# Group-norm chains shared between channel blocks and images, and some of them moved between stages, in a four-layer convolution kernel

## The chip, the cores and the metric

One core of a Trainium2 chip runs the whole network in one launch, in float32. The metric is device time in microseconds (us). Five engines run side by side, each through its own queue in order: PE (matmul; its weight loads are shown as PEld), DVE (vector), ACT (activation), POOL (GpSimd) and SP (only issues DMAs here). An engine waits for another by semaphore, and an instruction that waits holds up all that is queued behind it on its engine.

## The reference

Four layers, each of the form x = x + layer(groupnorm(x)), on x of shape (4, 256, 56, 56). Layers 0 and 2 are involutions, layer 1 is two 3x3 convolutions, layer 3 is a gate. What the change touches is the group norm:

```python
def _gn(v, G=32, eps=1e-5):
    g = v.reshape(B_, G, C_ // G, H_, W_)
    m = jnp.mean(g, axis=(2, 3, 4), keepdims=True)
    s = jnp.var(g, axis=(2, 3, 4), keepdims=True)
    return ((g - m) / jnp.sqrt(s + eps)).reshape(v.shape)

x = x + _L0_conv_ref(_gn(x), ...)   # involution: 7x7 kernels of every pixel, made by two 1x1 products
x = x + _L1_conv_ref(_gn(x), ...)   # conv3x3, bn, relu, conv3x3, bn, relu(x + h)
x = x + _L2_conv_ref(_gn(x), ...)   # involution with batch norms
x = x + _L3_conv_ref(_gn(x), ...)   # x * sigmoid gate of the channel + x * real DFT of the channel mean
```

A group is 8 channels of one image, so the mean and variance of one image and one block of 128 channels are 16 groups on 128 partitions.

## The kernel before

**Units.** A unit is one image and one block of 128 channels; there are 8 in a layer, unit u = 2 * image + block. An involution works through them one by one. Each unit has two stages. The *tap stage* (`tap_matrices`) has 32 steps: PE makes products of the span weights with the bottleneck's output (L594) into one of four two-bank PSUM buffers, and DVE (L612, two steps of three) or ACT (L605, every third step, those with n % 3 == 2) moves them with a bias into `kt`. The *column stage* has 7 columns: PE applies `kt` to the windows of the column (`apply`, L636), ACT and DVE combine the parts (L649 or L651, L656), the residual is added (POOL L661 in layer 0, DVE L663 in layer 2), PE transposes the next strip of the image (L408), and POOL or ACT makes the strip after that (L393, L391).

**Chains.** The group norm of one unit is a chain, the generator `norm_steps` (L212 to L236): `bn_aggr` of the statistics (DVE L216), a matmul that averages the means over 8 channels (PE L219), copy, subtract, square, add (DVE L222 to L227, four instructions in one step), a second matmul (PE L230), + eps (DVE L150), to the power -0.5 (POOL L151), and the shift (DVE L234): six steps, every operand 128 x 1. Each matmul takes one of the four PSUM buffers until DVE has read it. There are 32 chains, 8 for each of the four norms, and norm n + 1 of a unit needs the sums that layer n's columns leave behind (`column_sums`, L1106).

**Order.** All instructions of a layer keep the order in which the program writes them, on each engine (`in_order`). What is done beside a stage is placed by hand: `hooks[n]` is called after tap step n, `late[tx]` after column tx, and one call advances a generator by one step. Before the change, the chains stand like this:

- Layer 0, units 1 to 7: the last column's sums of the unit before at hook 1, its chain for norm 1 at hooks 2, 6, 7, 11, 12, 13.
- Layer 0, units 1, 3, 5 (block 1 of images 0 to 2): also the chain for norm 0 of the next image's block 0, at hooks 15, 19, 20, 24, 25, 26; the statistics for it (`sums`, L361) come one to a column in the column stage before. The next image's block 1 has its chain in columns 1 to 3 of units 1, 3, 5, and `bottleneck` of the next image follows there.
- Layer 1 (`conv_layer`): unit 7's chain for norm 1 at the start, and for norm 2 of images 0 to 2 two chains each, one per block, stepped through the second convolutions by `in_groups`.
- Layer 2, units 1 to 7: the chain for norm 3 of the unit before at hooks 2, 6, 7, 11, 12, 13, and `channel_mean` of that unit at hooks 13 (DVE L697, L708) and 17 (PE L716, L719). Units 1 and 2 also hold the chains for norm 2 of the last image, at hooks 15 to 26.
- Layer 2, units 3, 5, 7: POOL gate chunks (`gate_chunk`, L804 to L817) of the image before at hooks 14, 18, 22, 26. Units 2, 4, 6 have `gate_factors` at hooks 24 to 31.

Of the kernel before, what the change touches and what calls it, by code (L numbers as in the profile page):

```python
# [10 lines left out]
F32 = mybir.dt.float32  # L11
# [5 lines left out]
P = 128  # L17
# [56 lines left out]
def net_kernel(  # L74
# [70 lines left out]

    mhalf = const.tile([P, NB], F32, name="mhalf")
    nc.gpsimd.memset(mhalf, -0.5)
# [56 lines left out]

    norm_sb = const.tile([P, 4, B, 2, NB], F32, name="norm_sb")
    norms = [[[norm_sb[:, i, b, k, :] for k in range(2)] for b in range(B)] for i in range(4)]

# [3 lines left out]

    def norm_steps(st, one_bank, layer, b, cb):  # L212

        rstd, shift = (t[:, cb : cb + 1] for t in norms[layer][b])
        mv = small.tile([P, 2], F32, name="mv")
        nc.vector.bn_aggr(mv, st)  # L216
        yield
        ps = one_bank()
        nc.tensor.matmul(ps[:, 0:1], gavg_sb, mv[:, 0:1], start=True, stop=True)  # L219
        yield  # L220
        gm = small.tile([P, 1], F32, name="gm")
        nc.vector.tensor_copy(gm, ps[:, 0:1])  # L222

        d = small.tile([P, 1], F32, name="d")
        nc.vector.tensor_sub(d, mv[:, 0:1], gm)
        nc.vector.tensor_mul(d, d, d)
        nc.vector.tensor_add(d, d, mv[:, 1:2])  # L227
        yield
        ps = one_bank()
        nc.tensor.matmul(ps[:, 0:1], gavg_sb, d, start=True, stop=True)  # L230
        yield
        rsqrt_eps(rstd, ps[:, 0:1], GN_EPS)
        yield
        nc.vector.scalar_tensor_tensor(shift, gm, -1.0, rstd, ALU.mult, ALU.mult)  # L234
        yield

    redn_of = {}
# [63 lines left out]
    def involution_layer(layer, xin, xout, red, span, sb, xs_of, ahead=None, pending=None):  # L301

        with ExitStack() as es:
# [24 lines left out]
            if layer == 0:  # L328
                load(0, 0, (2, 2, 2, 1))
                load(0, 1, (2, 2, 2, 1))  # L330

                nc.scalar.activation(norm_sb[:, 3, B - 1, 1, :], mhalf, AF.Sigmoid)
            z_sb = wpool.tile([P, G // 2, ZN], F32, name="z_sb")
# [163 lines left out]
            def begin():  # L497
# [25 lines left out]
                steps(sums0, NCHUNK)  # L523
                norm = norm_steps(sums_of[0, 0], lambda: bank, 0, 0, 0)
                steps(norm, 2)
# [9 lines left out]
                steps(sums1, NCHUNK - 4)  # L535
                norm = norm_steps(sums_of[0, 1], lambda: bank, 0, 0, 1)

# [425 lines left out]

            def norm_of(layer, b, cb, st):
                return norm_steps(st, one_bank, layer, b, cb)

# [52 lines left out]
            for u, (b, cb) in enumerate(units):  # L1019
                hooks = hooks0 if u == 0 else {}  # L1020
                if prev is not None:
                    pb, pc, st, last_sums = prev
                    hooks.setdefault(1, []).append(last_column(last_sums))
                    place(hooks, norm_of(layer + 1, pb, pc, st), (2, 6, 7, 11, 12, 13))
                    if layer == 2 and u < 3:
                        g = norm_of(2, B - 1, u - 1, pending[1][u - 1])
                        place(hooks, g, (15, 19, 20, 24, 25, 26))
                    if layer == 2:
                        place(hooks, channel_mean(pb, pc), (13, 17))
                        if pc == 1:  # L1030
# [16 lines left out]
                if layer == 0 and cb == 1 and b + 1 < B:  # L1047
                    place(hooks, norm_of(0, b + 1, 0, sums_of[b + 1, 0]), (15, 19, 20, 24, 25, 26))

# [13 lines left out]
                if b + 1 < B:  # L1063
                    if layer == 0:
                        g = sums(b + 1, cb)
                        if cb == 0:
                            for tx in range(NTX):
                                late[tx].append(step(g))
                        else:
# [3 lines left out]
                            def norm_last():  # L1073
                                yield from norm_of(0, b + 1, 1, sums_of[b + 1, 1])

# [14 lines left out]
                if layer == 2 and b > 0:  # L1090
                    if cb == 0:
                        late[0] += [lambda b=b, j=j: load_sf(b - 1, j) for j in range(2)]
                    for tx in range(1, 6) if cb == 0 else range(NTX - 2):
                        late[tx] += [next_load, next_gate]
                if last_image and cb == 0:
                    for tx in range(6):
# [28 lines left out]
            if layer == 2:  # L1125
                run(last_normed(b, 0))
                bank = one_bank()
                mean, norm = last_mean(b, bank), norm_steps(st, lambda: bank, 3, b, cb)
                warm(16, ident_sb)
# [54 lines left out]
    def conv_layer(xin, xout, st, ahead):  # L1184
        with ExitStack() as es:
# [613 lines left out]
            def in_groups(g):  # L1799

                for n in (0, 0, 1, 1, 1, 0, 1, 1, 1):
                    for _ in range(n):
                        next(g, None)
                    yield
# [47 lines left out]

            tail1, tail2, slow = [], [], [in_groups(norm_steps(st, lambda: spare[0], 1, B - 1, NB - 1))]
            for s, (conv, i) in enumerate(order):
# [47 lines left out]
                else:  # L1902
# [60 lines left out]
                    if i % 3 == 0 and i > 0:  # L1963

                        slow += [in_groups(norm_steps(sums_of[i // 3 - 1][co], lambda: spare[0], 2, i // 3 - 1, co)) for co in range(NB)]
                    if nxt == (2, n_chunks - 1):
                        after[2].append(ahead)
                    between = [[] for _ in range(NB)]
                    for n, g in enumerate(slow[-NB:]):
                        between[n].append(step(g))  # L1970
# [86 lines left out]
```

## Time and profile before

| what | us |
|---|---|
| three timed runs | 1674.44, 1679.3, 1685.94 (median 1679.3) |
| the profiled execution, its own time | 1677.15 |
| its span, first to last instruction | 1675.3 |
| layer 0: first tap step to last column | 44 to 505 |
| layer 1 between the involutions | 505 to 1139 |
| layer 2: first tap step to last column | 1139 to 1642 |

A line of the profile gives an engine, a line of the kernel, the operation, and the tile it writes <- the tiles it reads. In a timeline the first two numbers are the start and the length in us, x is how many instructions were merged, and the square brackets give how long the engine had been idle and who ended that. A float32 matmul is two records, so a tap step of six products has twelve.

### The profile page before, as it was taken

The numbers are of one execution on the slowest core, as the hardware profiler recorded it, in microseconds if no ns is written. First come the engines' busy times: TensorE is split into PE (matmuls) and PEld (weight loads), VectorE is DVE, ScalarE is ACT, GpSimd is POOL, SyncE is SP. The second block draws the span as 40 slices with busy tenths as digits, with TensorE's granted clock in tenths as the row PEclk, the third lists the DMA queues.
The fourth block names the chain that finished last, engine by engine and source line by source line (L and its number), as shares of the span: only waits on it lengthen the run. The fifth ranks groups of instructions, "written<-read, shape, count | busy, mean of one in ns | idle before, by whom it ended". The sixth has DMA issues, their size and how long they took to land.

```text
span 1675.3 us, 57542 instructions
## 1 busy us (share of the span) xinstructions
PE 1601.8 (96%) x24640; PEld 1449.8 (87%) x24640; DVE 1333.5 (80%) x2451; ACT 1010.1 (60%) x2203; POOL 557.1 (33%) x774
## 2 busy tenths in 40 slices
PE   6999999999999999999999999988999899899898
PEld 4998998998888899899999999968888878788776
DVE  2686787787668988999999999986867777777775
ACT  2655555556446566676666666427776576676654
POOL 2134223322422343433333333100001581581571
PEclk9999999999998999999999999998999999999996
DMA  2354445444558977987888788653544774873752
GB/s 92 121 184 120 157 148 178 135 149 137 180 169 264 169 138 149 200 184 162 173 170 169 146 174 164 144 163 124 171 135 153 226 218 154 244 210 125 209 169 104
DMA packets 102876, 275.68 MB, mean 165 GB/s; under 512 B 15877, under 2 KB 43790, under 8 KB 98910
## 3 DMA queue, kind: packets, MB, share of 16 engines
q0 software_dynamic: 43856, 106.25, 30.8%
q1 hardware_dynamic: 57726, 164.48, 30.5%
q8 instruction: 195, 3.19, 0.8%
q10 hardware_dynamic: 1040, 1.26, 0.3%
q14 instruction: 59, 0.48, 0.1%
HBM read 95.07 MB, written 49.15 MB: 86 GB/s over the span
## 4 chain that ended last, share of the span: by engine, by line
PE 63%; DVE 16%; issue 7%; DMA 6%; ACT 5%; POOL 2%; SPq 1%; ACTq 0%; POOLq 0%; DVEq 0%
PE mm L1569 18%; PE ps L594 15%; PE ps L636 13%; PE mm L1554 7%; DVE kt L612 6%; DMA xw<-xw 4%; DVE un L656 3%; PE ps L408 3%; PE ps L470 1%; DVE st L1106 1%; ACT hp L489 1%; DVE xs L663 1%; DMA xs<-v 1%; ACT xw L420 1%; PE ps L719 1%
## 5 line engine op out<-in xcount | busy, mean ns | idle before, releaser
L636 PE MATMUL ps<-kt,xw 126*32 126x48 f32 (+1 forms) x12544 | 382.3, 236 | 21.9 <-DMA xw<-xw 9.4
L636 PEld LDWEIGHTS ps<-kt,xw 126*32 126x32 f32 (+1 forms) x12544 | 343.1, 122 | 68.0 <-issue 44.0
L594 PE MATMUL ps<-hp,z_sb 64*126 64x133 f32 x6144 | 384.9, 279 | 9.6 <-DVE kt L612 5.6
L594 PEld LDWEIGHTS ps<-hp,z_sb 64*126 64x126 f32 x6144 | 364.8, 186 | 26.0 <-DVE kt L612 7.7
L612 DVE TENSOR_TENSOR kt<-ps,zb_sb 126x798 f32<-126x798 f32 x352 | 333.2, 981 | 60.2 <-PE ps L594 48.8
L605 ACT ACTIVATE kt<-ps,zb_sb 126x133 f32<-126x133 f32 x960 | 280.3, 441 | 110.4 <-PE ps L594 110.4
L1569 PE MATMUL mm<-xs,u_sb 128*128 128x140 f32 (+2 forms) x1664 | 208.6, 278 | 1.7 <-DMA xs<-v 1.7
L1569 PEld LDWEIGHTS mm<-xs,u_sb 128*128 128x128 f32 x1664 | 199.4, 191 | 2.1 <-issue 1.7
L1554 PE MATMUL mm<-v,u_sb 128*128 128x280 f32 (+2 forms) x864 | 194.2, 383 | 2.0 <-DVE hp L1585 2.0
L1554 PEld LDWEIGHTS mm<-v,u_sb 128*128 128x128 f32 x864 | 162.2, 190 | 27.7 <-issue 2.4
L656 DVE SCALAR_TENSOR_TENSOR un<-ps,s,un 128x240 f32<-128x240 f32 x224 | 102.5, 457 | 88.1 <-ACT un L651 84.1
L656 DVE SCALAR_TENSOR_TENSOR un<-ps,par_sb,un 128x240 f32<-128x240 f32 x224 | 97.8, 456 | 82.5 <-ACT un L649 78.4
L1537 POOL DMA_DIRECT2D xs<-v x100 | 96.9, 1006 | 173.9 <-ACT xs L1536 161.2
L661 POOL TENSOR_TENSOR xs<-un,xs 128x240 f32<-128x240 f32 x112 | 72.2, 665 | 217.2 <-DVE un L656 217.2
L151 POOL TENSOR_TENSOR norm_sb<-norm_sb,mhalf 128x1 f32<-128x1 f32 x32 | 19.5, 609 | 344.0 <-DVE norm_sb L150 344.0
L420 ACT COPY xw<-ps 126x896 f32<-126x896 f32 x112 | 101.3, 905 | 40.9 <-PE ps L408 21.8
L649 ACT ACTIVATE un<-ps,par_sb 128x240 f32<-128x240 f32 x112 | 50.2, 448 | 120.0 <-PE ps L636 111.5
L408 PE MATMUL ps<-ident_sb,strip_sb 128*126 128x128 f32 x784 | 112.8, 285 | 6.3 <-POOL strip_sb L393 2.2
L651 ACT ACTIVATE un<-ps,bn_t,s 128x240 f32<-128x240 f32 x112 | 60.0, 538 | 92.0 <-PE ps L636 84.0
L408 PEld LDWEIGHTS ps<-ident_sb,strip_sb 128*126 128x126 f32 x784 | 85.7, 143 | 17.6 <-issue 3.9
L1569 PE MATMUL mm<-v_sb,u_sb 128*128 128x140 f32 (+2 forms) x688 | 94.2, 279 | 1.8 <-ACT u_sb L1316 1.8
L1536 ACT ACTIVATE xs<-v 128x560 f32<-128x560 f32 (+2 forms) x100 | 61.7, 628 | 49.5 <-DVE v L1481 41.6
(325 smaller groups left out, 2437.4 us busy)
## 6 DMA issues: line engine op xcount, KB each, us to landing
xw<-xw SPq DMA_DIRECT2D x224, 252.0 KB
xw<-xw SPq DMA_DIRECT2D x224, 126.0 KB
xs<-x POOLq DMA_DIRECT2D x24, 560.0 KB, 6.9
x<-xs POOLq DMA_DIRECT2D x8, 1568.0 KB, 8.1
xs<-x SPq DMA_DIRECT2D x8, 1568.0 KB
xs<-v POOLq DMA_DIRECT2D x44, 280.0 KB, 4.5
xs<-v POOLq DMA_DIRECT2D x42, 252.0 KB, 4.3
xs<-in_x_dram SPq DMA_DIRECT2D x6, 1568.0 KB
```

The costliest lines, as they stand in the source:

```text
L408: nc.tensor.transpose(ps[:Q, k * P : (k + 1) * P], flat[:, k * Q : (k + 1) * Q], ident_sb)
L420: nc.scalar.copy(xw[:, :NSB, :], ps[:Q, : NSB * P].rearrange("q (n c) -> q n c", n=NSB))
L594: nc.tensor.matmul(ps[:Q, i, k * NT : (k + 1) * NT], z_sb[i * R : (i + 1) * R, cb * GB // 2 + gp, z0 : z0 + Q], hp[i * R : (i + 1) * R, py ...
L605: nc.scalar.activation(kt[:, g0 + i, pb, :, k], ps[:Q, i, k * NT : (k + 1) * NT], AF.Identity, bias=zb_sb[:, cb * GB + g0 + i, p0 + k : p0 ...
L612: nc.vector.tensor_tensor(kt[:, g0 : g0 + 2, pb], ps[:Q, :, : PB * NT].rearrange("q i (k t) -> q i t k", k=PB), zb_sb[:, cb * GB + g0 : cb ...
L636: nc.tensor.matmul(v[m * j : m * j + m, i, :, k * TP : (k + 1) * TP], xw[:, window(ty), m * j : m * j + m], kt[:, ng * j : ng * j + ng, :, ...
L656: nc.vector.scalar_tensor_tensor(part, o[e], s, part, ALU.mult, ALU.add)
L661: nc.gpsimd.tensor_tensor(dst, u, dst, ALU.add)
L1536: nc.scalar.mul(t[:, at], v[:, below], -1.0)
L1537: nc.gpsimd.dma_start(t[:, at], v[:, at], accum_op=ALU.add)
L1554: nc.tensor.matmul(ps, *position(u, v, ci, dy, k, co, n), start=(j == 0), stop=(j == NB * 3 - 1))
L1569: nc.tensor.matmul(ps[:, bank, co * m : (co + 1) * m], u[ci][:, co * P : (co + 1) * P], v2[:, : n // 2, ci * WT : (ci + 1) * WT], start=(c ...
```

## The change

All chains work on several units at once if asked: the statistics of all 8 units stand in one tile `mv_sb`, the scales and shifts of one norm are contiguous over the units, and a chain takes a range u0:u1. Each small operation is now a step of its own (nine steps instead of six); where the six old steps are wanted, `by_counts` bundles them again.

```diff
-    norm_sb = const.tile([P, 4, B, 2, NB], F32, name="norm_sb")
+    norm_sb = const.tile([P, 4, 2, B * NB], F32, name="norm_sb")
+    mv_sb = const.tile([P, 2, B * NB, 2], F32, name="mv_sb")
...
+    def norm_steps(sts, one_bank, layer, u0, u1):
+        rstd, shift = (norm_sb[:, layer, k, u0:u1] for k in range(2))
+        mean, var = (mv_sb[:, layer % 2, u0:u1, k] for k in range(2))
+        for u, st in sts.items():
+            aggregate(st, layer, u)
         yield
         ps = one_bank()
-        nc.tensor.matmul(ps[:, 0:1], gavg_sb, mv[:, 0:1], start=True, stop=True)
+        nc.tensor.matmul(ps[:, :n], gavg_sb, mean, start=True, stop=True)
         yield
...
         nc.vector.tensor_copy(gm, ps[:, :n])
+        yield
         nc.vector.tensor_sub(d, mean, gm)
+        yield
         nc.vector.tensor_mul(d, d, d)
+        yield
         nc.vector.tensor_add(d, d, var)
         yield
...
+    def by_counts(g, counts):
+        for n in counts:
+            for _ in range(n):
+                next(g, None)
+            yield
```

In the involutions:

```diff
-                    hooks.setdefault(1, []).append(last_column(last_sums))
-                    place(hooks, norm_of(layer + 1, pb, pc, st), (2, 6, 7, 11, 12, 13))
-                    if layer == 2 and u < 3:
-                        g = norm_of(2, B - 1, u - 1, pending[1][u - 1])
-                        place(hooks, g, (15, 19, 20, 24, 25, 26))
+                    hooks.setdefault(5 if layer == 0 else 1, []).append(last_column(last_sums))
                     if layer == 2:
-                        place(hooks, channel_mean(pb, pc), (13, 17))
+                        place(hooks, norm_of(3, {u - 1: st}, u - 1, u), (2, 6, 8, 9, 10, 11, 13, 15, 16))
+                        place(hooks, channel_mean(pb, pc), (17, 18))
+                    else:
+                        hooks.setdefault(8, []).append(lambda st=st, u=u: aggregate(st, layer + 1, u - 1))
...
                 if layer == 0 and cb == 1 and b + 1 < B:
-                    place(hooks, norm_of(0, b + 1, 0, sums_of[b + 1, 0]), (15, 19, 20, 24, 25, 26))
+                    place(hooks, first, (5,))
...
                         if cb == 0:
-                            for tx in range(NTX):
+                            for j in range(NCHUNK + 1):
+                                late[j // 2].append(step(g))
+                            def norm_first():
+                                yield from norm_of(0, {u + 2: sums_of[b + 1, 0]}, u + 2, u + 3)
+                            g = first = norm_first()
+                            for tx in (3, 4, 5, 5, 5, 5, 6, 6):
                                 late[tx].append(step(g))
...
                 if last_image and cb == 0:
+                    g = by_counts(norm_of(1, {}, 0, u), (1, 1, 4, 1, 1, 1))
+                    for tx in range(1, 7):
+                        late[tx].append(step(g))
+                if layer == 2 and u == 0:
+                    g = by_counts(norm_of(2, dict(enumerate(pending[1], NB * (B - 1))), NB * (B - 1), NB * B), (1, 1, 4, 1, 1, 1))
+                    for tx in range(1, 7):
+                        late[tx].append(step(g))
```

So norm 1 of units 0 to 5 becomes one chain in the columns of unit 6, and units 6 and 7 share one in layer 1; in layer 1 the two blocks of an image share a chain for norm 2, and the two chains of the last image become one in the columns of unit 0 of layer 2:

```diff
-                        slow += [in_groups(norm_steps(sums_of[i // 3 - 1][co], lambda: spare[0], 2, i // 3 - 1, co)) for co in range(NB)]
+                        u = NB * (i // 3)
+                        sts = dict(enumerate(sums_of[i // 3 - 1], u - NB))
+                        slow.append(in_groups(norm_steps(sts, lambda: spare[0], 2, u - NB, u)))
...
-                    for n, g in enumerate(slow[-NB:]):
+                    for n, g in enumerate(slow[-1:]):
```

32 chains become 22.

## The prediction

> **What bounds the kernel now.** I read the page's busy table and the chain of waits first:
>
> ```profile
> PE 1601.8 (96%) x24640; PEld 1449.8 (87%) x24640; DVE 1333.5 (80%) x2451; ACT 1010.1 (60%) x2203; POOL 557.1 (33%) x774
> ...
> PE 63%; DVE 16%; issue 7%; DMA 6%; ACT 5%; POOL 2%; SPq 1%; ACTq 0%; POOLq 0%; DVEq 0%
> PE mm L1569 18%; PE ps L594 15%; PE ps L636 13%; PE mm L1554 7%; DVE kt L612 6%; DMA xw<-xw 4%; DVE un L656 3%; PE ps L408 3%; PE ps L470 1%; DVE st L1106 1%; ACT hp L489 1%; DVE xs L663 1%; DMA xs<-v 1%; ACT xw L420 1%; PE ps L719 1%
> ```
>
> PE sets the end nearly everywhere, so an edit is worth what it takes out of PE's row or out of waits of PE. Only in the tap stages does DVE (L612) stand beside it in the chain. So next I cut the span into tap stages, from the first L594 to the first L636 (busy time of each engine by stretch; first number the length). The first three are units 2, 3 and 4 of layer 0, the last unit 3 of layer 2:
>
> ```profile
> 164.20:188.97 24.77, 24.62 (x396) 23.79 (x396) 22.65 (x33) 18.42 (x61) 3.40 (x5) 1.00 0.47 166
> 217.66:244.27 26.61, 25.95 (x401) 24.59 (x400) 24.09 (x41) 18.43 (x61) 3.93 (x6) 1.00 0.49 168
> 280.35:305.12 24.77, 24.62 (x397) 23.79 (x396) 22.67 (x33) 18.43 (x61) 3.38 (x5) 1.00 0.46 164
> ...
> 1325.20:1353.05 27.85, 26.99 (x419) 24.43 (x418) 24.42 (x39) 20.54 (x64) 14.05 (x21) 1.00 0.59 198
> ```
>
> Units 2 and 4 hold one chain, unit 3 two: the trace has the experiment in it. A second chain costs 26.61 - 24.77 = 1.84 us. PE's timeline of unit 4 shows where one goes:
>
> ```profile
> 280.35 5.12 PE L594 MATMUL ps<-hp,z_sb 64*126 64x133 f32 x84
> 285.40 0.38 PE L219 MATMUL ps<-mv,gavg_sb 128*128 128x1 f32 x2
> 285.94 3.69 PE L594 MATMUL ps<-hp,z_sb 64*126 64x133 f32 x60 [0.15 <-DVE kt L612]
> 289.56 0.38 PE L230 MATMUL ps<-d,gavg_sb 128*128 128x1 f32 x2
> 289.87 14.39 PE L594 MATMUL ps<-hp,z_sb 64*126 64x133 f32 x240
> 304.20 0.98 PE L408 MATMUL ps<-ident_sb,strip_sb 128*126 128x128 f32 x7
> ```
>
> L219 to the next L594 is 0.54 us (in it a wait for DVE to free a buffer, since the chain holds one of four), L230 to the next 0.31, and the steps around them are slower.
>
> **Layer 0, tap stages.** Without a chain: layer 2's first tap stage has none, and its gapless run of 20 steps from 1151.75 to 1165.64 gives 13.89 / 20 = 0.695 us a step. 32 of them are 22.2; about 0.2 for switching weights at both ends and 0.84 for the transposes that stand before L636 make 23.3. So a lone chain costs 24.77 - 23.3 = 1.45 us. Seven stages (units 1 to 7) lose it: 10.2. Three (units 1, 3, 5) lose a second one: 3 x 1.84 = 5.5. Sum **-15.7**. What stays on DVE: the last column's sums (0.62, now hook 5), `bn_aggr` (0.34, hook 8), in three units one shift (0.16). DVE was busy for 22.67 of 24.77; without six small operations (about 1.0) it needs 21.7 of 23.3, so it has room, but little. I charge 0.1 a stage, **+0.7**; the bounds are 0 and the whole 0.96 of DVE time, which I don't take because in unit 4 the same two instructions stand at hooks 1 and 2 and L594 runs on without a gap to step 6.
>
> **Layer 0, columns.** Three chains (next image, block 0) and the six-unit chain go there. The trace has such a chain already, that of the next image's block 1. Three columns in a row, without a chain, with L219, with L230:
>
> ```profile
> 251.37:255.50 4.13, 4.13 (x119) 3.73 (x119) 4.03 (x10) 1.74 (x3) 2.28 (x3) 1.00 0.61 187
> 255.50:260.29 4.79, 4.29 (x127) 4.00 (x121) 3.91 (x12) 1.80 (x3) 2.16 (x3) 1.00 0.65 206
> 260.29:264.70 4.41, 4.28 (x128) 4.00 (x121) 2.61 (x11) 1.80 (x3) 2.77 (x5) 1.00 0.55 162
> ```
>
> 0.66 + 0.28 = 0.94 us. The block 0 chain has its second matmul behind the last column, ahead of tap step 0, where the buffer wait (0.50 before L636 at 257.10) may come twice: bounds 0.94 and 1.45, I take 1.2. 3 x 1.2 + 0.95 = **+4.5**. Six columns of operands instead of one change nothing: the instructions' length is fixed cost (a 128x1 DVE operation takes 0.15, L716 with 1 column 0.18). The sums (L361), now two to a column, cost nothing: the column at 251.37 holds three and is 4.13 long. If that cover went, 7 x 0.6 us a unit in three units would show. POOL gets three L151 of 0.56 behind strips (0.99 each) in columns where it is busy for 2.3 of 4.1. Layer 0: -15.7 + 0.7 + 4.5 = **-10.5**.
>
> A rule to weigh against the row of L219: the Trainium skill ("TensorE: Matmul & The Clock Gate", section "Wait — 56ns, not 53.3ns?") gives small matmuls a floor of about 25 ns from start to start; by it a chain's four records would be 0.1 us of PE and ten chains about 1 us, an estimate that speaks against any visible gain. The stages' difference of 1.84 us says that a chain's price is the switch and the buffer, not the matmul.
>
> **Layer 1.** Three of seven chains go. The norm matmuls there take 0.14 us from start to next start (L219 at 630.76, L1554 again at 630.90). 3 x 2 x 0.14 = **-0.8**. DVE's and ACT's evictions sometimes wait for such a matmul in their bank (L1770 3.1 us in all 8, L1766 1.8); if half of it counted, another -1.
>
> **Layer 2.** Units 1 and 2 lose a second chain. Unit 1: steps 19 to 31 with it take 10.32 (1213.08 to 1223.40), 13 x 0.695 + 0.1 without, so -1.2; unit 2 (31.05 from the transposes on) against units 4 and 6 (30.43, 30.24) -0.7. The chain in unit 0's columns +0.95. Together **-1.0**.
>
> The chain for norm 3 stays in seven tap stages, now with a step for each operation. L219 stays at hook 6 behind the same burst of sums and `bn_aggr`, so its wait stays. The four small DVE operations in a row end 0.7 us before anyone needs them; spreading them gives 0 to 0.25 a unit, I take 0.
>
> What I do charge is `channel_mean`, moved from hooks 13 and 17 to 17 and 18. Unit 3 of layer 2, timeline:
>
> ```profile
> 1337.48 0.15 DVE L150 TENSOR_SCALAR norm_sb<-ps 128x1 f32<-128x1 f32 x1
> 1337.54 0.98 DVE L612 TENSOR_TENSOR kt<-ps,zb_sb 126x798 f32<-126x798 f32 x1
> 1337.71 0.56 POOL L151 TENSOR_TENSOR norm_sb<-norm_sb,mhalf 128x1 f32<-128x1 f32 x1 [14.79 <-DVE norm_sb L150]
> ...
> 1338.44 0.17 DVE L234 SCALAR_TENSOR_TENSOR norm_sb<-gm,norm_sb 128x1 f32<-128x1 f32 x1
> 1338.64 0.27 DVE L697 TENSOR_SCALAR first<-xs,norm_sb 128x1 f32<-128x1 f32 x1
> 1338.83 0.81 DVE L708 TENSOR_SCALAR mean<-cmean,norm_sb 128x32 f32<-128x32 f32 x2
> ```
>
> Here hook 13's operations end at 1339.64, 2.46 us after step 13's matmuls ended (1337.18); in units without gate chunks L708 takes 0.38 instead of 0.81 and it is 2.02. PE then has four steps until L716 needs them. After the change the same sequence (+ eps at hook 15, a DVE step, shift, `first`, two `mean`) sits at hooks 15 to 17, and L716 comes two steps (1.47 us) after step 16: PE waits 2.02 - 1.47 = 0.55 in units 1, 2, 4, 6 and 1.0 in 3, 5, 7, plus about 0.1 for the signal. In 3, 5, 7 it takes the place of a wait that goes (L719 behind L612, 0.3). 4 x 0.65 + 3 x 0.8 = **+5.0**; bounds 0 (if DVE runs further ahead) and 7 x 1.2 = 8.4. Behind the waiting PE are the tap steps, and nothing else of PE's can go ahead. Layer 2 in all **+4.0**.
>
> A second rule, on 0.38 against 0.81: the Trainium skill ("SBUF — State Buffer", section "Who interferes with whom") has DVE and POOL lock each other out of a shared port pair; the rows of L708 agree in units with gate chunks, and by it the early gate chunk (below) could also hold DVE's small operations by up to a whole POOL instruction.
>
> **Sum.** -10.5 - 0.8 + 4.0 = -7.3. On the profiled execution (1677.15): 1669.9. The median of the timed runs is 2.1 above that execution, which would make 1672.0; I say **1671**.
>
> **Rivals.**
> *The whole gain (0.15).* DVE is ahead at hook 17, spreading pays 0.25 in seven units, layer 1's evictions pay 1: -15.7 + 3.8 - 1.0 - 1.8 - 1.8 = -16.5, 1660.7. For it: DVE waits for PE 0.50 just before L150 in these stages. Against: the chain eps, step, shift, mean is serial, whoever waits first.
> *DVE becomes the tap stage's bound (0.25).* In unit 4 DVE idles 2.1 of 24.77. If it needs that idle time to stay in step, a stage can't go under 21.7 + 2.1 = 23.8: 1.0 a stage instead of 1.45, 3.2 less gain, and the full 8.4 at `channel_mean`, 3.4 more: about -0.7, 1676.5. For it: L612 carries 6% of the chain of waits. Against: the gapless 20 steps, with the same 21 evictions.
> *Slower: the gate chunk stands in POOL's queue ahead of L151 (0.08).* In units 3, 5, 7 the chunk at hook 14 was behind the chain's L151 (hook 12); now it is ahead of it (hook 15). The chunk takes 5.2 us (L804 at 1338.24 to the end of L817 at 1343.41). If its data or buffers are late, L151 waits up to 5.2, DVE's shift at hook 16 with it, and behind the shift L612, and PE: 3 x 5 = 15, so -7.3 + 15 = +7.7, 1684.8. It decides as soon as the chunk ends later than L150 at hook 15. Against: POOL sat idle 14.79 us before L151 in unit 3, three times the chunk, which can now slide forward into it.
>
> The rest (0.52) is the forecast, 1666 to 1674. DMA waits in layer 2's columns (up to 1.4 each) shift with any change, and the three runs spread by 11.5; the range that holds 8 in 10 is 1660 to 1680, from the whole gain to the DVE case with a run's scatter. About 1% is what a measurement of this kernel can tell from no change: faster by more means under 1662.5, most of the first rival, 0.12; slower by more means over 1696, beyond all cases, 0.02; the rest 0.86.
>
> **What would show it.** Layer 0's tap stages at 23.3 to 23.5 all alike, with L594 gapless; columns with L219 4.8; in layer 2 an idle time of PE before L716, ended by DVE's `mean`, of 0.5 to 1.1. L151 in units 3, 5, 7 right after L150, with the chunk ended before: else the third rival. Wrong if L594 in layer 0 shows gaps ended by L612, or the tap stages keep 24 us and more.

## The result and the profile after

| | before | after | ratio, 95% interval |
|---|---|---|---|
| 13 timed runs of each, median (lowest to highest), us | 1681.48 (1674.44 to 1693.8) | 1668.47 (1661.16 to 1674.53) | 0.9921 [0.9901, 0.9941] |
| a second series, 16 and 7 runs | 1679.34 | 1669.48 | 0.9935 [0.9911, 0.9959] |
| the profiled executions shown here: own time; span | 1677.15; 1675.3 | 1671.08; 1669.1 | |

The kernel is about 0.7% faster. 1671 was forecast, 8.3 us under the median of 1679.3 known then; the medians fell by 13.0 and 9.9. The page of the changed kernel, busy time and chain of waits:

```profile
PE 1589.1 (95%) x24600; PEld 1445.2 (87%) x24600; DVE 1328.8 (80%) x2391; ACT 1010.3 (61%) x2203; POOL 551.5 (33%) x764
...
PE 69%; DVE 13%; ACT 6%; DMA 5%; issue 5%; POOL 2%; SPq 1%; ACTq 0%; POOLq 0%; DVEq 0%
PE mm L1601 20%; PE ps L611 18%; PE ps L653 14%; PE mm L1586 8%; DVE kt L629 3%; PE ps L425 3%; DMA xw<-xw 3%; DVE un L673 3%; PE ps L487 2%; ACT kt L622 1%; ACT hp L506 1%; ACT ph L1469 1%; PE ps L965 1%; PE ps L736 1%; PE ps L338 1%
```

Lines have moved by 17 or so: L594 is now L611 (tap products), L612 is L629 (DVE eviction), L605 is L622 (ACT eviction), L408 is L425, L230 is L240 (second norm matmul), L697 and L708 are L714 and L725 (`first` and `mean`), L716 and L719 are L733 and L736 (the two parts of `channel_mean` on PE). Forty PE records fewer are the ten chains. DVE's eviction fell from 6% to 3% of the chain, PE's tap products rose from 15 to 18%: the tap stages are PE's again.

Stretches of the changed kernel, tap stages of units 2, 3 and 4 of layer 0, and unit 3 of layer 2 (first the length, then busy time of PE, PEld, DVE, ACT, POOL with counts, granted clock, DMA share, GB/s):

```profile
161.79:185.14 23.35, 23.35 (x392) 23.05 (x391) 21.86 (x27) 18.43 (x61) 2.83 (x4) 1.00 0.49 175
214.66:238.00 23.34, 23.34 (x391) 23.04 (x392) 21.72 (x28) 18.27 (x61) 3.28 (x5) 1.00 0.54 187
274.09:297.44 23.35, 23.35 (x392) 23.05 (x391) 21.87 (x27) 18.42 (x61) 2.83 (x4) 1.00 0.49 173
...
1319.80:1347.62 27.82, 26.69 (x418) 24.33 (x417) 23.54 (x37) 20.55 (x64) 18.34 (x27) 1.00 0.67 219
```

24.77, 26.61 and 24.77 have become 23.35 three times, and PE is busy for all of it. PE's timeline of unit 4 has one piece where there were five:

```profile
274.09 22.50 PE L611 MATMUL ps<-hp,z_sb 64*126 64x133 f32 x384
296.53 0.98 PE L425 MATMUL ps<-ident_sb,strip_sb 128*126 128x128 f32 x7
```

Where the time went over the whole program, cut at PE's instructions (us; three profiles of the changed kernel, two of the kernel before, and two experiments told below). A convolution matmul's number counts PE's records in layer 1.

| stretch | before | | after | | | eps_only | layer0_only | mean difference | predicted |
|---|---|---|---|---|---|---|---|---|---|
| layer 0, first tap step to unit 7's columns | 431.7 | 434.0 | 421.4 | 420.7 | 420.8 | 419.1 | 420.5 | -11.8 | -10.5 |
| to the first convolution matmul | 42.9 | 42.1 | 47.3 | 41.6 | 44.4 | 43.0 | 47.1 | +1.9 | 0 |
| convolution matmul 0 to 1200 | 187.9 | 188.1 | 191.5 | 191.3 | 189.1 | 188.2 | 192.9 | +2.6 | } |
| 1200 to 3300 | 274.4 | 274.5 | 272.6 | 272.6 | 273.3 | 272.6 | 275.1 | -1.6 | } -0.8 |
| 3300 to layer 2's first tap step | 158.3 | 158.3 | 158.3 | 159.7 | 159.7 | 159.8 | 160.9 | +0.9 | } |
| layer 2, to its last column | 502.5 | 498.9 | 500.2 | 498.6 | 501.9 | 501.1 | 497.2 | -0.5 | +4.0 |
| start and tail | 77.7 | 78.0 | 77.9 | 80.2 | 79.1 | 79.5 | 79.0 | +1.2 | 0 |

The differences are those of the means of the columns before and after; together -7.4. Layer 0 brings the whole gain; a few us are lost in layer 1, in places that differ from run to run; layer 2 is the same within its own scatter.

### The profile page after: what moved, and what is told of

It is laid out like the page before. It is cut to its first block, busy times and chain, and to the rows that moved or that the text cites. A ratio compares the mean times of both kernels' runs of the same rounds, so it can differ in the third digit from the quotient of the medians.

```text
span 1669.1 us, 57385 instructions
## 1 busy us (share of the span) xinstructions
PE 1589.1 (95%) x24600; PEld 1445.2 (87%) x24600; DVE 1328.8 (80%) x2391; ACT 1010.3 (61%) x2203; POOL 551.5 (33%) x764
## 3 DMA queue, kind: packets, MB, share of 16 engines
q0 software_dynamic: 43856, 106.25, 31.1%
## 4 chain that ended last, share of the span: by engine, by line
PE 69%; DVE 13%; ACT 6%; DMA 5%; issue 5%; POOL 2%; SPq 1%; ACTq 0%; POOLq 0%; DVEq 0%
PE mm L1601 20%; PE ps L611 18%; PE ps L653 14%; PE mm L1586 8%; DVE kt L629 3%; PE ps L425 3%; DMA xw<-xw 3%; DVE un L673 3%; PE ps L487 2%; ACT kt L622 1%; ACT hp L506 1%; ACT ph L1469 1%; PE ps L965 1%; PE ps L736 1%; PE ps L338 1%
## 5 line engine op out<-in xcount | busy, mean ns | idle before, releaser
L611 PE MATMUL ps<-hp,z_sb 64*126 64x133 f32 x6144 | 377.1, 278 | 10.6 <-ACT kt L622 3.4
L629 DVE TENSOR_TENSOR kt<-ps,zb_sb 126x798 f32<-126x798 f32 x352 | 333.5, 982 | 66.5 <-PE ps L611 55.0
L611 PEld LDWEIGHTS ps<-hp,z_sb 64*126 64x126 f32 x6144 | 363.8, 186 | 23.9 <-ACT kt L622 9.5
L622 ACT ACTIVATE kt<-ps,zb_sb 126x133 f32<-126x133 f32 x960 | 280.4, 441 | 92.8 <-PE ps L611 92.8
L666 ACT ACTIVATE un<-ps,par_sb 128x240 f32<-128x240 f32 x112 | 50.2, 448 | 126.2 <-PE ps L653 112.4
L425 PE MATMUL ps<-ident_sb,strip_sb 128*126 128x128 f32 x784 | 111.4, 282 | 6.1 <-ACT hp L506 3.6
L425 PEld LDWEIGHTS ps<-ident_sb,strip_sb 128*126 128x126 f32 x784 | 84.6, 141 | 17.3 <-POOL strip_sb L410 3.9
L1601 PEld LDWEIGHTS mm<-v_sb,u_sb 128*128 128x128 f32 x688 | 88.2, 193 | 3.8 <-ACT u_sb L1348 2.3
```

What stands on the lines that cost most here:

```text
L425: nc.tensor.transpose(ps[:Q, k * P : (k + 1) * P], flat[:, k * Q : (k + 1) * Q], ident_sb)
L611: nc.tensor.matmul(ps[:Q, i, k * NT : (k + 1) * NT], z_sb[i * R : (i + 1) * R, cb * GB // 2 + gp, z0 : z0 + Q], hp[i * R : (i + 1) * R, py ...
L622: nc.scalar.activation(kt[:, g0 + i, pb, :, k], ps[:Q, i, k * NT : (k + 1) * NT], AF.Identity, bias=zb_sb[:, cb * GB + g0 + i, p0 + k : p0 ...
L629: nc.vector.tensor_tensor(kt[:, g0 : g0 + 2, pb], ps[:Q, :, : PB * NT].rearrange("q i (k t) -> q i t k", k=PB), zb_sb[:, cb * GB + g0 : cb ...
L1601: nc.tensor.matmul(ps[:, bank, co * m : (co + 1) * m], u[ci][:, co * P : (co + 1) * P], v2[:, : n // 2, ci * WT : (ci + 1) * WT], start=(c ...
```

## The experiments

Each kernel is the changed one with the edit shown, with one profile; where a ratio is given, also timed beside the kernel before.

**1 and 2. The two kernels once more.** No edit: how much of the first two profiles repeats.

> The changed kernel once more, for a second profile. Stage by stage the first profile of it gained 10.3 us in layer 0 but lost 6.2 us between the last column stage of layer 0 and layer 2, while the timed runs gained 13 us. Theory: that loss belongs to this one execution, since it has stretches of half clock at 553 and 690 and a longer one at 498 that the profile of before doesn't have. Then the stretch from the last column stage of layer 0 to the first tap step of layer 2 is 660 to 664 us here, with no half clock in it after the transition, and the execution 1662 to 1668. Rival: sharing the chains makes layer 1 longer; then it is again 668 to 671 us.

> The kernel before once more, for a second profile. Theory (the stages repeat): layer 0's tap stages again at 24.8 us with one chain and 26.6 with two, within 0.1. The stretch of layer 1 can differ by the half clock alone. Rival: the stages scatter by more than 0.5 us from one execution to the next; then the gain in the tap stages can't be read from one profile.

The changed kernel took 1666.65, the kernel before 1675.75. Layer 0's tap stages repeat within 0.02 us with one exception (26.46 where the first profile has 26.58). Layer 1 does not: in `after_again` it took 665.1 from unit 7's columns to layer 2's first tap step, between the two expectations (669.6 in the first profile, 663.4 and 663.1 in the two of before). So the loss in layer 1 is not the same from run to run. One such place, PE's timeline of the first profile of the changed kernel:

```profile
685.93 1.12 PE L1601 MATMUL mm<-v_sb,ux 128*128 128x140 f32 x8
688.95 3.28 PE L1601 MATMUL mm<-xs,u_sb 128*128 128x140 f32 x16 [1.91 <-DMA xs<-v]
```

PE waits 1.91 us for a transfer (1.49 before), and the 16 records after it, 2.15 long before, take 3.28, most of it at half the granted clock. The same wait was 1.2 in `before_again`, 1.3 in `eps_only`, 2.7 in `after_again` and 4.35 in `layer0_only`, where the convolutions of layer 1 have two chains an image as before.

**3. Where layer 2's tap stages wait.** The stages with norm 3 should have come out longer by a wait before `channel_mean`'s matmuls. In the changed kernel two waits are seen in unit 3, PE's timeline:

```profile
1330.49 0.38 PE L240 MATMUL ps<-d,gavg_sb 128*128 128x1 f32 x2
1330.96 2.32 PE L611 MATMUL ps<-hp,z_sb 64*126 64x133 f32 x36
1333.76 1.64 PE L611 MATMUL ps<-hp,z_sb 64*126 64x133 f32 x24 [0.48 <-ACT kt L622]
1335.77 0.24 PE L733 MATMUL ps<-one,mean 128*32 128x1 f32 x8 [0.37 <-DVE mean L725]
1335.86 1.68 PE L736 MATMUL ps<-xs,mean 128*32 128x448 f32 x14
```

The second is the predicted one, at 0.37. The first, three steps after the second norm matmul, stands in all seven units: step 17 starts 1.33 us after step 16 instead of 0.68. The record names ACT's eviction. All engines around it, same kernel:

```profile
1332.65 0.99 DVE L629 TENSOR_TENSOR kt<-ps,zb_sb 126x798 f32<-126x798 f32 x1 [0.84 <-PE ps L611]
1332.75 0.96 ACT L622 ACTIVATE kt<-ps,zb_sb 126x133 f32<-126x133 f32 x3
...
1333.55 0.15 DVE L150 TENSOR_SCALAR norm_sb<-ps 128x1 f32<-128x1 f32 x1
1333.62 0.98 DVE L629 TENSOR_TENSOR kt<-ps,zb_sb 126x798 f32<-126x798 f32 x1
...
1333.76 1.64 PE L611 MATMUL ps<-hp,z_sb 64*126 64x133 f32 x24 [0.48 <-ACT kt L622]
1333.79 0.56 POOL L151 TENSOR_TENSOR norm_sb<-norm_sb,mhalf 128x1 f32<-128x1 f32 x1 [7.67 <-DVE norm_sb L150]
```

ACT's and DVE's L150 end within 0.01 us of each other (1333.71 and 1333.70). The theory: it is + eps (L150), at hook 15 behind step 15's eviction, that holds the fourth PSUM buffer since hook 13. The edit moves it one hook forward:

```diff
-  place(hooks, norm_of(3, ...), (2, 6, 8, 9, 10, 11, 13, 15, 16))
+  place(hooks, norm_of(3, ...), (2, 6, 8, 9, 10, 11, 13, 14, 16))
```

> From the changed kernel: in layer 2 the + eps that reads the second norm matmul moves from hook 15 to hook 14, all else stays. Theory A (the buffer): step 17 of PE takes the PSUM buffer of that matmul and waits for the + eps, which hook 15 puts behind the eviction of step 15. Then step 16 to step 17 falls from 1.33 us to about 0.7 in all seven tap stages, and PE, which then comes sooner to the channel mean's matmuls, waits there for DVE instead, 0.5 us in units 1, 2, 4, 6 and 1.0 in units 3, 5, 7 (the wait of the prediction). The tap stages of layer 2 stay within 0.3 us of the changed kernel's (30.75 in units 4 and 6). Rival B: step 17 waits for ACT's eviction of step 14, which the record names; then step 16 to 17 stays at 1.33.

Step 17 came 0.68 us after step 16: the late + eps was the cause of the wait. PE's timeline of unit 3 in this kernel, and ACT's eviction of step 14:

```profile
1324.41 0.38 PE L240 MATMUL ps<-d,gavg_sb 128*128 128x1 f32 x2
1324.89 3.76 PE L611 MATMUL ps<-hp,z_sb 64*126 64x133 f32 x60
1330.04 0.21 PE L733 MATMUL ps<-one,mean 128*32 128x1 f32 x5 [1.40 <-DVE mean L725]
```

```profile
1325.88 1.75 ACT L622 ACTIVATE kt<-ps,zb_sb 126x133 f32<-126x133 f32 x6 [1.05 <-PE ps L611]
```

The first wait is gone, L611 runs for five steps (14 to 18), and `channel_mean`'s wait is 1.40, in units 5 and 7 too; in units 1, 2, 4 and 6 it is 0.63. The stages of units 4 and 6 stay what they were (30.78 and 30.77): whichever wait stands first, PE comes to the same late `mean`.

That + eps was the cause does not make the name in the record wrong. Step 17 starts at 1327.04 here (three steps after 1324.89), while ACT empties step 14's buffer until 1327.63, so step 17 has another buffer. It is probably the one that + eps has just freed; with + eps a hook later step 17 would get step 14's, which ACT takes 1.75 us to empty. `probe_held` below shows by its times that a wait of this kind ends with ACT.

**4 and 5. Both waits taken away.** + eps and the shift one hook sooner, `channel_mean`'s DVE part at hook 15, its PE part at 19 or 20:

```diff
-  place(hooks, norm_of(3, ...), (2, 6, 8, 9, 10, 11, 13, 15, 16))
-  place(hooks, channel_mean(pb, pc), (17, 18))
+  place(hooks, norm_of(3, ...), (2, 6, 8, 9, 10, 11, 13, 14, 15))
+  place(hooks, channel_mean(pb, pc), (15, 19))    # eps_sooner;  (15, 20) in mean_at_20
```

> From the changed kernel: in layer 2 + eps at hook 14, the shift at hook 15, the channel mean's vector part at 15 and its matmuls at 19 (17 and 18 before). Theory A (PE waits for the buffer at step 17 and for DVE before the channel mean): both waits go; the tap stages fall by 0.6 us in units 1, 2, 4, 6 and by 1.0 in 3, 5, 7, to 30.1 in units 4 and 6 and to about 27.0 in unit 3; 5.4 us in all, 1663 by the median. Rival: DVE's own load sets these stages; then moving the steps leaves the stages within 0.2 us and the time at 1668.

> As eps_sooner (+ eps at hook 14, shift and the vector part of the channel mean at 15), but the channel mean's matmuls at hook 20 instead of 19. Theory A (four PSUM buffers in turn): at hook 19 the pair of banks of L736 is the buffer of step 17, which ACT empties 1.75 us long, so PE waited 0.4 us there; at hook 20 it is that of step 18, which DVE empties in 0.98. Then no wait of PE over 0.1 us is left from step 13 to the channel mean; the tap stages are 30.1 us in units 2, 4, 6 (30.75 in the changed kernel), 27.6 in unit 1, 26.9 to 27.1 in unit 3. Rival (DVE's load sets these stages): they stay at 30.5 and above, as with hook 19.

`eps_sooner`: 1668.37, 0.993 [0.9907, 0.9952]; its stages of units 2, 4, 6 took 30.49, 30.51 and 30.76 (30.76, 30.75, 30.75 in the changed kernel), where about 30.1 was expected. Both waits were gone and new ones stood in `channel_mean`. In units 1, 2, 4 and 6 L736 started 0.48 after L733 instead of 0.08, when ACT had finished an eviction: behind step 19 the pair takes the buffer of step 17, which ACT empties over 1.75 us (every third step, six pieces), not DVE in 0.98. In units 3, 5 and 7 PE waited 0.3 before L733 for an eviction of DVE. `mean_at_20`, whose pair takes a DVE step's buffer: 30.18, 30.54, 30.54. The first is close to the 30.1 expected; the other two hold a wait before step 4, which has nothing to do with the edit (unit 4 of the kernel before, 30.43, has it too). In units 3, 5 and 7 PE waits 0.3 before step 20, since the DVE part now stands ahead of step 16's eviction. 1664.63, 0.9894 [0.9873, 0.9915]: the lowest ratio, with an interval that overlaps those of the change itself.

**6. Layer 0 alone.** Norm 2 and norm 3 go back to two chains and six steps, with the hooks of before, the chain in unit 0's columns of layer 2 goes (and there are three buffers for two small tiles, since two chains are under way at once):

```diff
-  place(hooks, norm_of(3, ...), (2, 6, 8, 9, 10, 11, 13, 15, 16)); place(hooks, channel_mean(pb, pc), (17, 18))
+  place(hooks, by_counts(norm_of(3, ...), (1, 1, 4, 1, 1, 1)), (2, 6, 7, 11, 12, 13))
+  if u < 3: place(hooks, by_counts(norm_of(2, ...), (1, 1, 4, 1, 1, 1)), (15, 19, 20, 24, 25, 26))
+  place(hooks, channel_mean(pb, pc), (13, 17))
...
-  slow.append(in_groups(norm_steps(sts, lambda: spare[0], 2, u - NB, u)))
+  slow += [in_groups(norm_steps({v: st}, lambda: spare[0], 2, v, v + 1)) for v, st in sts.items()]
```

> The part of the change in layer 0 alone; layers 1 and 2 have the places and the number of chains of the kernel before, but for the chain that units 6 and 7 share at the start of layer 1. Theory: layer 0's tap stages 23.35 us, columns as in the changed kernel, so the whole gain of the change, 10 us, is here: 1668 by the median, as fast as the changed kernel within 3 us. Layer 2's tap stages are those of before (28.6, 31.0, 27.85, 30.4). Rival: the other two parts bring a third of the gain or more; then it is 1672 or slower.

1666.92, 0.9904 [0.9876, 0.9933]: as much as the whole change. What was done in layers 1 and 2 adds nothing that these runs can tell. Its convolutions from matmul 1200 to 3300 take 275.1, against 272.6 with shared chains.

**7, 8 and 9. What a chain costs in a tap stage.** Three probes put parts of a chain back into the seven tap stages of layer 0 that had become plain. `probe_held` adds two one-column matmuls, each read by DVE three steps later; `probe_pe` the same matmuls with no reader; `probe_dve` only six small DVE operations.

```diff
+  ps = one_bank(); nc.tensor.matmul(ps[:, 0:1], gavg_sb, gavg_sb[:, 0:1], ...)   # hooks 19, 24: probe_held, probe_pe
+  nc.vector.tensor_copy(t, ps[:, 0:1])                                          # hooks 22, 27: probe_held
+  nc.vector.tensor_sub(t, gavg_sb[:, 0:1], gavg_sb[:, 1:2])                     # hooks 20 (x4), 25, 26: probe_dve
```

> The changed kernel with an addition in layer 0's tap stages of units 1 to 7: at hooks 19 and 24 a matmul of gavg_sb by one of its columns into a PSUM buffer of its own, and 3 steps later a 128x1 copy out of it on DVE. Theory A: besides the switch (0.3 to 0.5 us each) PE waits for the buffer four allocations later, since the copy stands behind the eviction of step 22 and of step 27: 0.6 to 0.7 us each; the stages go from 23.35 to 25.3 to 25.8. Rival: a chain's price is DVE's time; two copies of 0.15 us make 23.7 at most.

> The changed kernel with an addition in layer 0's tap stages of units 1 to 7: DVE's six small operations of a chain alone (128x1 subtractions of constants), four at hook 20, one at 25, one at 26, no matmul. Theory A (PE's switch and buffer are a chain's price): the stages stay at 23.35 to 23.6. Rival (DVE's time is its price): six times 0.19 us, 24.3 to 24.5, or 1.1 us of the 1.4 that a chain cost.

> The changed kernel with an addition in layer 0's tap stages of units 1 to 7: at hooks 19 and 24 a matmul of gavg_sb by one of its columns into a PSUM buffer of its own that nothing reads, so that only PE's own order holds the buffer. With a copy out of it three steps later these cost 2.79 us a stage, 2 x 0.65 of it waits for the buffer. Theory A: what is left without them is the switch alone, 1.4 to 1.5 us, 24.8 us a stage, which is also what a lone chain cost before. Rival: the switch is small (two times the 0.31 us from such a matmul to the next step) and the rest was the buffer; then 24.0.

Tap stages 2 to 7 of layer 0: 23.35 in `probe_dve`, 24.56 in `probe_pe`, 26.14 in `probe_held`. Six DVE operations cost nothing. PE's timeline of unit 4, first `probe_pe`, then `probe_held`, and for `probe_held` one line of ACT's timeline and one of DVE's:

```profile
279.78 14.17 PE L611 MATMUL ps<-hp,z_sb 64*126 64x133 f32 x240
293.88 0.38 PE L1068 MATMUL ps<-gavg_sb 128*128 128x1 f32 x2
294.37 3.76 PE L611 MATMUL ps<-hp,z_sb 64*126 64x133 f32 x60
298.06 0.38 PE L1068 MATMUL ps<-gavg_sb 128*128 128x1 f32 x2
298.37 5.13 PE L611 MATMUL ps<-hp,z_sb 64*126 64x133 f32 x84
```

```profile
295.00 0.38 PE L1069 MATMUL ps<-gavg_sb 128*128 128x1 f32 x2
295.49 2.32 PE L611 MATMUL ps<-hp,z_sb 64*126 64x133 f32 x36
298.29 1.64 PE L611 MATMUL ps<-hp,z_sb 64*126 64x133 f32 x24 [0.48 <-ACT kt L622]
299.85 0.38 PE L1069 MATMUL ps<-gavg_sb 128*128 128x1 f32 x2
300.16 3.25 PE L611 MATMUL ps<-hp,z_sb 64*126 64x133 f32 x48
303.89 2.32 PE L611 MATMUL ps<-hp,z_sb 64*126 64x133 f32 x36 [0.48 <-ACT kt L622]
```

```profile
296.49 1.75 ACT L622 ACTIVATE kt<-ps,zb_sb 126x133 f32<-126x133 f32 x6 [1.05 <-PE ps L611]
```

```profile
298.97 0.15 DVE L1072 COPY probe<-ps 128x1 f32<-128x1 f32 x1
```

With no reader, 293.88 to 294.37 is 0.49 and 298.06 to 298.37 is 0.31, as in the kernel before (0.54 and 0.31); the step on either side is longer by about 0.1; together 1.21 a pair. About 0.1 of the 0.49 is a wait that ends with an eviction of ACT; the rest PE spends without waiting for anyone. With a reader three steps late there is one more gap for each matmul, three and four steps after it, and two steps start 1.33 after the step before instead of 0.68. The stage grows by 2.79, to more than the 25.3 to 25.8 expected: a late reader costs 0.79 (half of 26.14 - 24.56), 0.65 of it in the step that waits and the rest in the steps around it.

The expectation had PE wait for the copy out of the held buffer. The lines of ACT and DVE say otherwise: the copy (L1072) started at 298.97, 0.68 after step 23 had started at 298.29, and ACT's eviction of step 20 ended at 298.24. So the record's name is right. While one of the four buffers is held, three go round, and the two steps that wait, 23 and 29, come three behind ACT's steps 20 and 26. Layer 2's step 17, three behind ACT's step 14, has the same picture.

**10 and 11. `channel_mean` at hooks 16 and 20, and the change timed again beside it.**

```diff
+  place(hooks, norm_of(3, ...), (2, 6, 8, 9, 10, 11, 13, 14, 15)); place(hooks, channel_mean(pb, pc), (16, 20))
```

> As mean_at_20, but the vector part of the channel mean at hook 16 instead of 15. In mean_at_20 PE waited before step 20 (0.45 us in unit 3, 0.2 in units 2, 4, 6), because the vector part, 0.4 to 0.8 us, stood on DVE ahead of step 16's eviction, whose buffer step 20 takes. Theory A (buffers in turn, and who empties them): behind that eviction DVE is free anyway, since ACT empties step 17; the wait goes, and the tap stages are 30.2 to 30.4 us in units 4 and 6 (30.75 in the changed kernel), 27.6 in unit 1, 26.8 in unit 3. By the stages this is 4 us under the changed kernel: 0.989 of the kernel before, against 0.992. Rival: another wait comes in its place, stages as in mean_at_20 (30.5 in units 4 and 6).

> The changed kernel, timed beside mean_16_20 on the same chip: 0.992 of the kernel before, and slower than mean_16_20 by 0.2 to 0.3%. Its third profile has again 23.35 us in the plain tap stages of layer 0. Rival: the two can't be told apart.

Units 1, 2, 4 and 6 took 27.37, 30.08, 30.08 and 30.07, about 0.67 less than the changed kernel in 2, 4 and 6 and a little less than expected. Units 3, 5 and 7 missed it (28.53, 28.26, 29.96 against 27.83, 29.02, 28.84). From step 8 to step 20 they took 12.3 to 12.4 instead of 12.7; the rest of the difference lies in the steps before, with a gap of 1.53 of PE's own issue in unit 7. Unit 3 of this kernel, timeline of all engines:

```profile
1331.55 1.14 POOL L830 TENSOR_TENSOR gx<-gx,gn 128x448 f32<-128x448 f32 x1
1331.57 0.26 DVE L714 TENSOR_SCALAR first<-xs,norm_sb 128x1 f32<-128x1 f32 x1
1331.75 1.12 DVE L725 TENSOR_SCALAR mean<-cmean,norm_sb 128x32 f32<-128x32 f32 x2
1332.79 1.87 DVE L629 TENSOR_TENSOR kt<-ps,zb_sb 126x798 f32<-126x798 f32 x2
...
1333.82 1.70 PE L736 MATMUL ps<-xs,mean 128*32 128x448 f32 x14 [0.56 <-DVE kt L629]
```

Both L725 start while POOL's gate chunk (L830) runs and take 1.12 us instead of the 0.38 they take without it; the eviction behind them is late, and L736 waits 0.56 for its buffer. In time the two kernels can't be told apart: 0.9928 [0.9901, 0.9955] and 0.9935 [0.9911, 0.9959].

**12. Norm 0's chain back in the tap stages** of units 1, 3 and 5, the rest of the change kept:

```diff
-  place(hooks, first, (5,))
+  place(hooks, first, (15, 19, 20, 24, 25, 26))    # and no steps of it in the columns
```

> The changed kernel with the chain for norm 0 of the next image's block 0 back in the tap stages of units 1, 3, 5 at the old hooks (15 to 26). Theory: these stages rise by the price of a chain there, 1.4 to 1.85 us, to 24.8 to 25.2, and the columns of units 0, 2, 4 fall by the price there, 0.85; so moving three chains is worth 2 to 3 us in all, and the rest of layer 0's 10 us comes from sharing. Rival: the moved chains are half the gain, 5 us.

The three stages took 24.73 (23.35 to 23.52 without), the columns of unit 2 28.80 (29.5 to 30.2 in the kernels that have the chain there). Unit 0's columns, 29.84, lie among the others' 29.4 to 30.3 and say nothing. By unit 2 a chain costs 1.2 to 1.4 in a tap stage and about 0.7 to 0.85 in columns. To move it is worth some 0.5, so 1.5 for the three and not the 2 to 3 expected; to share it is worth all of it. The single run took 1668.3.

## Why the prediction was right, and where it was not

**Layer 0, tap stages: right.** -15.7 was predicted for removed chains and +0.7 for what stays on DVE, -15.0; the seven stages lost 15.2. The plain stage of 23.3, put together from layer 2's gapless run, came out at 23.35, and the 0.1 a stage for DVE's left-over is at most 0.05. The price was right and so was its reason in part: `probe_pe` shows 1.21 of a lone chain's 1.42 (24.77 - 23.35) with nobody reading, nearly all of it PE's own switching; the prediction's "the switch and the buffer" holds, with the buffer as the small part when DVE reads one step later, and 0.79 for each matmul when it reads three steps later. The rule weighed there (the Trainium skill, "TensorE: Matmul & The Clock Gate", section "Wait — 56ns, not 53.3ns?", a floor of 25 ns for small matmuls) does not price this case; the stages decide.

**Layer 0, columns: the mechanism right, the term mis-sized.** 1.2 was taken for a block 0 chain between 0.94 and 1.45; the columns of unit 2 grew by 0.82 in the first profile, and `first_in_taps` gives 0.7 there. The second buffer wait did not come. In single profiles the columns of unit 4 (29.47 to 31.58) hid this with gaps put down to issue; other profiles of kernels with the same columns have 29.5 to 32.3. Layer 0 in all: -10.3 in the first pair, -11.8 in the means, -10.5 predicted.

**Layer 1: the step that failed is "3 x 2 x 0.14 = -0.8".** From matmul 1200 to 3300 the convolutions alone take 272.6 to 273.3 instead of 274.4 and 274.5; in all eleven profiles with shared chains it is 272.6 to 274.1, and with two chains again (`layer0_only`) 275.1. Set side by side, matmul by matmul, the first pair shows where. Six norm matmuls are gone from the layer, and at each the lead grows by 0.22: 0.14 from start to start, as predicted, and 0.08 in the record behind it. So they bring 1.3, not 0.8. Four of the six stand in this stretch and bring 0.9 of its 1.8. The other 0.9 comes at three more places (0.21, 0.46 and 0.21), where PE starts on operands that DVE or a transfer has just delivered; the prediction had named a second gain of 1 and not taken it.

Layer 1 as a whole shows no gain. After matmul 3300 `eps_only` takes 1.5 us longer than the kernel before: DVE's statistics (L1779) wait 4.20 us for an accumulating transfer instead of 1.83, and behind them on DVE are the evictions that PE needs. Counted from matmul 3300, that transfer ended after 128.3 us in `eps_only` and after 126.7 in the kernel before. But it ended after 126.8 in the first profile of the changed kernel, after 126.2 to 128.7 in the eleven profiles with shared chains, and latest of all, after 129.1, in `layer0_only`. So sharing is not what holds it up; what does wasn't tried.

What else layer 1 and the way to it lost (+1.9 and +2.6 in the means) goes with waits of 1 to 4 us for transfers, some with stretches at half clock behind them. They differ between profiles of one kernel, and `eps_only` has no stretch at half clock among the convolutions up to 1110. `layer0_only`, with two chains an image in layer 1, took 676.0 from unit 7's columns to layer 2's first tap step, the longest of all fourteen profiles. So the shared chains of the convolutions are not needed for the loss; whether the rest of the change makes it more frequent is open.

**Layer 2: +4.0 predicted, nothing found in the layer's total; the stages show it, with the waits right in size and partly in another place.** "PE waits 2.02 - 1.47 = 0.55 in units 1, 2, 4, 6 and 1.0 in 3, 5, 7" before L716: in the changed kernel PE's waits in layer 2 that are new read like this (line, who ended them, us in total, times, longest):

```profile
PE ps L611 <- ACT kt L622: 3.4, 7, 0.5
...
PE ps L733 <- DVE mean L725: 1.1, 3, 0.4
```

and in `eps_only`, where the obstacle ahead is gone:

```profile
PE ps L733 <- DVE mean L725: 6.7, 7, 1.4
```

The predicted wait is there in all seven units, 0.63 and 1.40, as soon as nothing holds PE up before it. (0.65 and 1.1 were predicted; the 0.3 more in units 3, 5 and 7 is what `mean`'s two operations take there, 1.14 instead of 0.81.) What was overlooked is that + eps at hook 15 keeps the second norm matmul's buffer out of the round, so that step 17 waits: 0.65 in every unit, of which `mean`'s wait is then relieved.

What this costs is read from step 8 to the end of the stage, since a wait before step 4 and others like it come and go in steps 0 to 7. Units 3 and 4, the kernel before and then the changed kernel:

```profile
1332.43:1353.05 20.62, 20.39 (x324) 18.34 (x320) 17.29 (x28) 15.20 (x50) 14.05 (x21) 1.00 0.52 183
1396.66:1419.48 22.82, 22.67 (x342) 19.89 (x338) 17.79 (x33) 15.36 (x52) 1.11 (x2) 1.00 0.40 138
```

```profile
1326.21:1347.62 21.41, 20.46 (x323) 18.31 (x319) 17.20 (x28) 15.19 (x50) 12.65 (x18) 1.00 0.62 214
1390.64:1414.19 23.55, 22.82 (x341) 19.96 (x337) 17.78 (x33) 15.40 (x52) 1.11 (x2) 1.00 0.40 138
```

Unit 4 grew by 0.73 us and unit 3 by 0.79; 0.65 and 0.8 were predicted. Units 1 and 2, which lost their second chain as well, fell by 0.4 and 0.3, so that chain was worth about 1.2 and 1.0; 1.2 and 0.7 were predicted, the 0.7 too low because units 4 and 6, from which it was read, held the wait before step 4. Together the seven stages grew by 3.0 from step 8 on, where -1.9 + 5.0 = +3.1 was predicted. Spreading the four small operations gained nothing, as the prediction took it: `mean_16_20`, with nine steps and no wait, has 22.87 in unit 4, and the six-step chains of the kernel before and of `layer0_only` have 22.82. The chain in unit 0's columns shows too: 28.4 to 28.7 without it, 29.6 to 31.1 with it.

The layer's total hides this. In steps 0 to 7 the changed kernel's first profile is 2.1 shorter than that of the kernel before, the columns move by up to 3 us either way in both kernels, with waits for `xw`, and the two profiles of the kernel before differ by 3.6 in this layer. So the mean of -0.5 is mostly chance: the seven profiles that have layer 2 as in the changed kernel take 501.2 on average, the three without its edits 499.5. The timed runs can't tell either: `layer0_only`, without these edits, is as fast within its interval.

**The rivals.** DVE as the tap stage's bound did not come: DVE is busy for 21.87 of 23.35, so it kept its pace with 1.5 of idle time where the rival wanted 2.1, and six operations more (`probe_dve`) left 23.35. The gate chunk ahead of L151 did not come either: POOL had been idle for 7.67 us when L150 ended at 1333.70, and L151 started at 1333.79. What did come of the early chunk is the slowed L725: 0.38 without, 0.67 to 1.15 beside POOL's operations. That agrees with the Trainium skill ("SBUF — State Buffer", section "Who interferes with whom"), by which DVE and GpSimd share a pair of ports that one of them holds alone, and it was `mean_16_20` that ran into it. The whole gain (-16.5) was right on cheap columns and on layer 1's middle; but spreading paid nothing, `mean` was late, and layer 1 as a whole lost time.

**The sum.** -7.3 was predicted; in the means of the profiles it is -7.4 (1674.66 to 1667.26), and that they agree to 0.1 is luck: by those means layer 0 came out 1.3 better than predicted, layer 2 4.5 better, layer 1 with its approach and the ends 5.8 worse, and the last two are mostly scatter of a few profiles. Both profiled executions of the kernel before (1677.15, 1675.75) lie low among its timed runs; which stretch is longer in the others has no trace here and stays open.

## What to carry to other kernels

A stage that exists with one and with two copies of a thing prices that thing better than its instructions do: 0.38 us of norm matmul cost 1.4 in the tap stage. A small result in a ring of large buffers leaves fewer buffers for the rest, so read it within a step, and see which engine empties the buffer that the steps behind it get. Where a whole layer scatters, compare the part of a stage that repeats. When a predicted wait is missing, remove the one in front of it before calling the lateness wrong.

## What the hardware showed that was not expected

- Two 128x1 matmuls put among steps with other weights cost 1.21 us of PE with nobody reading them, though their records are 0.38 each; six 128x1 DVE operations in the same stage cost nothing.
- A PSUM buffer held for three steps cost PE 0.79 us, though PE did not wait for its reader: a step behind it waited until ACT had emptied a buffer, which takes ACT 1.75 us and DVE 0.98. Moving the reader (`eps_only`) took the wait away all the same.
- The two 128x32 operations of L725 took 0.38 us without POOL beside them and 0.67, 0.81 or about 1.13 with it.
- Some waits of PE of about 2 us in layer 1 are followed by 3.4 us at half clock. Three stretches of the changed kernel, the middle one right after PE's wait of 2.09 us (the column before the DMA share is the granted clock):

```profile
549.80:553.20 3.40, 1.40 (x12) 1.19 (x10) 3.30 (x7) 2.33 (x6) 1.14 (x1) 1.00 1.24 195
553.20:556.60 3.40, 3.31 (x14) 3.31 (x15) 3.27 (x7) 1.36 (x4) 2.21 (x2) 0.51 1.24 198
556.60:560.00 3.40, 3.40 (x30) 3.40 (x29) 3.30 (x8) 1.86 (x3) 1.98 (x3) 0.99 1.23 196
```

Waits of 1.5 and 1.8 at these places had no such stretch behind them, 1.91 and 2.09 had, and one of 2.11 in `eps_only` had none: the length alone does not decide it.
